# Layout of the per-pixel weights in DRAM: the eight rows of a column side by side, in place of the columns of a row

## The chip, the core and the metric

The kernel runs on one core of one Trainium2 chip. The metric is the device time of one execution, in microseconds (us). It is reported as the median of several runs; beside it stands one execution that was recorded by the hardware profiler, with its own time. A core has a tensor engine (PE, with its weight loads shown as PEld), a vector engine (DVE), a scalar engine (ACT), GpSimd (POOL) and SyncE (SP), which here only issues DMAs. Sixteen DMA engines carry all transfers. Each engine works through its own instructions in order and waits on semaphores.

## What is computed

Two layers on a batch of 32 images, 256 channels, 32x32 pixels, float32. Layer 0 is group norm, a 3x3 convolution with operands rounded to a half-precision format, bias, and a residual sum. Layer 1 is an involution: after a group norm, two 1x1 convolutions make for every pixel a 7x7 kernel for each of 16 groups of 16 channels, and that kernel is applied to the pixel's neighbourhood.

```python
x = x + _L0_conv_ref(_gn(x), weight, bias)            # 3x3, 256 -> 256
xn = _gn(x)
y = relu(batch_norm(einsum('oc,bchw->bohw', w1, xn))) # 256 -> 64
w = einsum('oc,bchw->bohw', w2, y) + b2               # 64 -> 16*49
w = w.reshape(b, 16, 49, H, W)
patches = 7x7 neighbourhoods of xn, (b, 16, 16, 49, H, W)
x = x + einsum('bgkhw,bgckhw->bgchw', w, patches)
```

## The kernel before

The 32 images go through a software pipeline written out by hand. The loop at the end of the function counts steps; an image takes 16 of them (`per = 2 * M`, M = 8), so that at a span of 1342.5 us an image costs about 42 us and a step about 2.6 us. Each stage of an image has a lag in steps (`due(n, lag)`): the front (group norms, convolution, first 1x1 convolution, transposes) runs 56 steps ahead, the per-pixel weights 18 steps ahead, and the sums of the involution at lag 0.

The involution is done on TensorE as products with band matrices. An image is cut into K = 4 bands of TR = 8 rows. A band's matrix needs the 7x7 weights laid out so that partition (r, j) holds, at a place that depends on j, the weights of pixel (row r, column j); the left and the right half of the row (SIDES = 2, JC = 16 columns each) lie behind one another. Getting there takes a trip through DRAM:

1. `weights` (L411) computes the weights of four rows in PSUM; DVE adds the bias and writes them into a ring in SBUF (`evict`, L435): partition = column, the rows as slots of the ring.
2. `scatter` (L476, on SP's queue) writes the ring into the DRAM tensor `wd`, one DMA for each of the 7 column offsets `dj`: 32 columns x 8 rows, pieces of WB = 160 elements (640 B). There are 7 x 4 x 32 = 896 of these DMAs, in two parts of a band (`part` 0: 4 of them, `part` 1: 3, one step later). A piece goes to column p + dj, tap place 6 - dj, so that afterwards the seven pieces of one column and row lie in a run of WPIX = 1128 elements (4512 B).
3. `load_bands` (L497) reads it back: for each j of 0 to 15 one DMA that takes 8 rows x 2 sides, runs of up to 1128 elements, into the 8 partitions `band[j::16]`. j = 0 and 1 go by SP's queue, the other 14 by POOL's. The order in a band is `ORDER`, j = 15 last. A band is loaded 9 steps before its sums; there are three band buffers (NBAND = 3).
4. `sums` (L522) multiplies with the band on PE, `add_windows` (L538) adds to x on DVE, `store` (L543) writes out by SP's queue. `load_x` (L106) fetches images by SP's queue too.

At the beginning three DMAs by SP's queue (L191) put zeros into the parts of `wd` that no scatter writes: the 8 spare elements at the end of every run, and the border columns. Their source is a band buffer that POOL has set to zero.

`wd` before is `[H, S, WPIX]`, with S = 38 columns (32 and a border of 3 on each side): the columns of a row follow one another at 4512 B, and the rows at ROW = S * WPIX elements, 171 KB.

Of the kernel before, what the change touches and what calls it, by code (L numbers as in the profile page):

```python
# [9 lines left out]
F32 = mybir.dt.float32  # L10
# [4 lines left out]
B, C, H, W = 32, 256, 32, 32  # L15
# [5 lines left out]
K1, PAD1 = 7, 3  # L21
# [18 lines left out]
TR = RG * XR  # L40
SIDES = 2
JC = W // SIDES
K = H // TR
# [8 lines left out]
V = 2  # L52
A = G // V
WB = G * WIN
PAD = V * (TR - XR)
WPIX = K1 * WB + PAD
SW = K1 * G
S = H + 2 * PAD1
T = 4
TW = P // T  # L60
PAIR = 3 * GC
PAIRS = G // 2
ROW = S * WPIX
WR = 4
NBAND = 3
BY_SYNC = (0, 1)
# [12 lines left out]
def tile_quant_conv_then_involution(  # L79
# [10 lines left out]
    nc = tc.nc  # L90
# [6 lines left out]
    dram = ctx.enter_context(tc.tile_pool(name="dram", bufs=1, space=bass.MemoryType.DRAM))  # L97
# [44 lines left out]
    bands = [const.tile([P, SIDES, WINC * WB + PAD], F32, name=f"band_{i}") for i in range(NBAND)]  # L142
# [5 lines left out]


    w_sb = const.tile([P, 2, RING, A, WIN, V], F32, name="w_sb")  # L150
    wd = dram.tile([H, S, WPIX], F32, name="wd")
    acc = [ps_acc.tile([P, RG, NT], F32, name=f"acc_{d}") for d in range(SIDES)]

    wq = const.tile([P, CH, K0 * K0, C], F16, name="wq")
# [23 lines left out]
    nc.vector.tensor_sub(bn_shift, bn[:, 1:2], bn_shift)  # L178


    for col, cols, at, n in (
        (0, S, K1 * WB, PAD),
        (PAD1, PAD1, 0, PAD1 * WB),
        (W, PAD1, (K1 - PAD1) * WB, PAD1 * WB),
    ):
        to = bass.AP(
            tensor=wd.tensor,
            offset=wd.offset + col * WPIX + at,
            ap=[[ROW, H], [WPIX, cols], [1, n]],
        )  # L190
        nc.sync.dma_start(to, bands[NBAND - 1][:H, 0, :n].unsqueeze(1).to_broadcast([H, cols, n]))  # L191

    def quantize_weights(kh):

# [270 lines left out]
    def scatter(b, k, part):  # L465

        at = (b * H + k * TR) % RING
        for dj in range(part, K1, 2):
            t, e = divmod(dj, 2)
            to = bass.AP(  # L470
                tensor=wd.tensor,
                offset=wd.offset + k * TR * ROW + dj * WPIX + (K1 - 1 - dj) * WB,
                ap=[[WPIX, TW], [ROW, TR], [1, WB]],
            )
            rows = w_sb[t * TW : (t + 1) * TW, e, at : at + TR]
            nc.sync.dma_start(to, rows.rearrange("p s a r v -> p s (a r v)"))  # L476

    def load_bands(b, k):

        band = bands[(b * K + k) % NBAND]  # L480
        side = WINC * WB + PAD
        for i, j in enumerate(ORDER):
            cut = max(0, PAD1 - j)
            n = (K1 - cut) * WB + PAD
            src = bass.AP(
                tensor=wd.tensor,
                offset=wd.offset + k * TR * ROW + (j + PAD1) * WPIX + cut * WB,
                ap=[[ROW - V, TR], [(W - 1 - 2 * j) * WPIX - cut * WB, SIDES], [1, n]],
            )
            to = band[j::JC]  # L490
            to = bass.AP(
                tensor=to.tensor,
                offset=to.offset + (j + cut) * WB,
                ap=[to.ap[0], [side + (JC - 1 - 2 * j - cut) * WB, SIDES], [1, n]],
            )
            queue = nc.sync if j in BY_SYNC else nc.gpsimd
            queue.dma_start(to, src)  # L497
# [56 lines left out]
    with tc.manual_schedule():  # L554
        fronts = {}
        for n in range(FRONT, B * per + 2):
# [30 lines left out]
            for part in range(2):  # L587
                b, i = due(n, -LEAD + 1 + part)
                if b is not None and i % 2 == 0:
                    for k in range(K):  # L590
                        if i // 2 == min((k + 1) * TR // WR, H // WR - 1):
                            scatter(b, k, part)
# [5 lines left out]
            if b is not None and i % 4 == 0:  # L598
                load_bands(b, i // 4)
# [38 lines left out]
```

## Time and profile before

| | |
|---|---|
| median of 3 runs | 1353.44 us (1347.35 to 1364.31) |
| the profiled execution, its own time | 1344.24 us |
| its span, first to last instruction | 1342.5 us |
| mean granted clock of TensorE | 0.982 |
| PE busy | 1253.6 us (93%) |
| POOL busy | 1014.4 us (76%) |
| DVE busy | 818.8 us (61%) |
| ACT busy | 733.3 us (55%) |
| DMA packets | 360724, 361.85 MB, mean 270 GB/s |

The profiled execution is 0.7% under the median of the runs. "Busy" leaves out the issuing of DMAs on SP; for POOL it includes it (L497 POOL). In a list of waits a line names the engine that waited and its line, then the engine or DMA that ended the wait; the numbers are the microseconds in total, how often, and the longest. In the chain, which is followed back from the last instruction, each piece is what the piece after it had waited for. "SPq" is SP's queue, where each DMA issue has a duration of its own.

### The profile page before, as it was taken

Reading aid. Unit: us, or ns where it says so; the run is one execution under the profiler, and the core shown is the slowest. Engines: PE = TensorE matmul, PEld = TensorE weight load, DVE = VectorE, ACT = ScalarE, POOL = GpSimd, SP = SyncE. Lnnn points to the kernel's source line nnn. Section 1 sums busy time; section 2 is a strip of 40 time slices with the busy share of each in tenths; the row PEclk is TensorE's granted clock in tenths of the full one; section 3 lists DMA queues with packets and bytes.
Section 4 is the critical chain, followed back from the end, with each engine's and each line's share of the span. In section 5 each row is a group of like instructions: output and inputs, shape, how many; then the busy total and the mean of one; then the engine's idle time right before and its main releaser. Section 6 shows DMA issues by size and latency. Waiting matters only on the chain.

```text
span 1342.5 us, 65799 instructions
## 1 busy us (share of the span) xinstructions
PE 1253.6 (93%) x27648; PEld 763.7 (57%) x27648; DVE 818.8 (61%) x2539; ACT 733.3 (55%) x1731; POOL 1014.4 (76%) x1818
## 2 busy tenths in 40 slices
PE   5899999999999999999999999999999999999665
PEld 2356566565555655556655556666555566556454
DVE  3466666565666665656665666766666666666442
ACT  5775656455656556556545655655556564553300
POOL 9067878777787778777778787788777877788785
PEclk9999999999999999999999999999999999999987
DMA  6089999999999999999999999999999999999995
GB/s 228 11 237 295 271 293 293 279 266 281 272 286 282 291 285 270 283 263 280 293 282 283 270 288 282 293 297 296 281 288 275 277 284 290 271 281 266 278 274 166
DMA packets 360724, 361.85 MB, mean 270 GB/s; under 512 B 75056, under 2 KB 304752, under 8 KB 359152
## 3 DMA queue, kind: packets, MB, share of 16 engines
q1 hardware_dynamic: 278512, 229.38, 56.8%
q0 software_dynamic: 81920, 128.28, 33.9%
q8 instruction: 220, 3.60, 1.1%
q14 instruction: 72, 0.59, 0.1%
HBM read 176.60 MB, written 180.76 MB: 266 GB/s over the span
## 4 chain that ended last, share of the span: by engine, by line
PE 60%; DMA 23%; POOL 7%; issue 3%; ACT 3%; DVE 2%; SPq 1%; POOLq 0%; DVEq 0%; ACTq 0%
PE pc L332 25%; PE acc L522 19%; DMA band<-wd 17%; PE pw L411 11%; POOL band L497 7%; DMA wd<-w_sb 6%; PE pt L396 3%; PE py L377 3%; ACT junk L214 1%; SPq L476 1%; DVE w_sb L435 1%; DMA x<-in_x 1%; ACT xn L273 0%; SPq L497 0%; ACT xq L273 0%
## 5 line engine op out<-in xcount | busy, mean ns | idle before, releaser
L497 POOL DMA_DIRECT2D band<-wd x1792 | 980.3, 549 | 315.7 <-DMA band<-wd 182.0
L435 DVE TENSOR_TENSOR w_sb<-pw,late_sb 128x224 f32<-128x224 f32 (+7 forms) x1280 | 330.4, 322 | 419.5 <-PE pw L411 419.2
L332 PE MATMUL pc<-xq,wq 128*128 128x496 f16 (+3 forms) x2304 | 535.2, 379 | 20.3 <-ACT xq L273 18.3
L522 PE MATMUL acc<-band,pixels 64*32 64x190 f32 (+1 forms) x16384 | 426.6, 332 | 51.8 <-DMA band<-wd 42.7
L522 PEld LDWEIGHTS acc<-band,pixels 64*32 64x32 f32 x16384 | 304.7, 107 | 159.7 <-issue 81.1
L332 PEld LDWEIGHTS <-wq 128*128 128x128 f16 x2304 | 206.7, 98 | 316.1 <-issue 102.7
L411 PE MATMUL pw<-late_sb,y 64*32 64x224 f32 (+1 forms) x8192 | 288.9, 333 | 10.8 <-issue 9.4
L538 DVE TENSOR_TENSOR x<-acc,x 128x380 f32<-128x380 f32 (+1 forms) x512 | 262.0, 512 | 32.2 <-PE acc L522 23.2
L411 PEld LDWEIGHTS pw<-late_sb,y 64*32 64x32 f32 x8192 | 186.5, 106 | 38.1 <-issue 21.0
L400 ACT COPY pixels<-pt 128x512 f32<-128x512 f32 x128 | 73.7, 576 | 228.6 <-PE pt L396 228.6
L214 ACT ACTIVATE junk<-x 128x512 f16<-128x512 f32 (+1 forms) x192 | 146.4, 763 | 14.7 <-DVE x L348 12.2
L214 ACT ACTIVATE junk<-x,mean 128x1024 f16<-128x1024 f32 x128 | 147.1, 1149 | 4.3
L245 ACT ACTIVATE s<-back,eps 128x2 f32<-128x2 f32 x64 | 18.9, 296 | 178.6 <-DVE back L230 178.6
L346 DVE TENSOR_SCALAR q<-pc 128x512 f16<-128x512 f32 x128 | 87.2, 681 | 17.6 <-PE pc L332 17.6
L273 ACT ACTIVATE xn<-x,off,rstd 128x512 f32<-128x512 f32 x128 | 96.2, 800 | 0.0
L348 DVE SCALAR_TENSOR_TENSOR x<-q,early_sb,x 128x512 f32<-128x512 f16 x128 | 94.2, 736 | 0.3
L396 PEld LDWEIGHTS pt<-ident,xn 128*128 128x128 f32 x512 | 63.9, 142 | 26.3 <-issue 2.5
L396 PE MATMUL pt<-ident,xn 128*128 128x128 f32 x512 | 78.0, 275 | 0.1
L273 ACT ACTIVATE xq<-x,off,rstd 128x1024 f16<-128x1024 f32 x64 | 75.7, 1227 | 0.0
L235 ACT ACTIVATE mean<-back 128x2 f32<-128x2 f32 x64 | 12.6, 196 | 101.4 <-DVE back L230 101.4
L377 PE MATMUL py<-xn,early_sb 128*64 128x512 f32 x256 | 62.2, 606 | 0.9 <-ACT xn L273 0.9
L224 DVE STREAM_TRANSPOSE across<-sums 128x32 f32<-128x32 f32 x128 | 26.3, 205 | 33.6 <-ACT junk L214 32.4
(40 smaller groups left out, 369.3 us busy)
## 6 DMA issues: line engine op xcount, KB each, us to landing
wd<-w_sb SPq DMA_DIRECT2D x896, 160.0 KB
band<-wd POOLq DMA_DIRECT2D x1664, 70.5 KB, 4.6
x<-in_x SPq DMA_DIRECT2D x64, 512.0 KB
out<-x SPq DMA_DIRECT2D x64, 512.0 KB
band<-wd POOLq DMA_DIRECT2D x128, 60.5 KB, 4.6
band<-wd SPq DMA_DIRECT2D x128, 50.5 KB
band<-wd SPq DMA_DIRECT2D x128, 40.5 KB
band<-in_w SPq DMA_DIRECT2D x2, 1152.0 KB
```

Source lines behind the costliest of these rows:

```text
L214: nc.scalar.activation(junk[:, n0:n1], src[:, h, n0:n1], func, bias=bias, accum_out=self.sums[:, i : i + 1])
L273: nc.scalar.activation(dst, src, AF.Identity, bias=self.off[:, one], scale=self.rstd[:, one])
L332: nc.tensor.matmul(pc.rearrange("p (r c) -> p r c", c=W)[:, r0 - nt * RT : r1 - nt * RT, c0:c1], wq[:, kh, k, mh * P : (mh + 1) * P], xq[: ...
L346: nc.vector.tensor_scalar(q, pc, F16_MAX, -F16_MAX, ALU.min, ALU.max)
L348: nc.vector.scalar_tensor_tensor(xt[:, mh, cols], q, bias_sb[:, mh : mh + 1], xt[:, mh, cols], ALU.add, ALU.add)
L377: nc.tensor.matmul(py[i * CR : (i + 1) * CR], w1_sb[:, kh, :], px[:, :, i], start=kh == 0, stop=kh == CH - 1,)
L396: nc.tensor.transpose(pt[:, i, h * P : (h + 1) * P], xn[:, h, (m + i) * P : (m + i + 1) * P], ident)
L411: nc.tensor.matmul(pws[i][t * TW : (t + 1) * TW, : dj.stop - dj.start, r], y_sb[b % 2][half, (r0 // 2 + r) * W : (r0 // 2 + r + 1) * W], w ...
L435: nc.vector.tensor_tensor(to, of[:, :, d0:d1], bias[:, :, d0:d1], ALU.add)
L497: queue.dma_start(to, src)
L522: nc.tensor.matmul(at[t * TW : (t + 1) * TW, h, :, f - top : l - top], px[p, a, v * GC : v * GC + TW], of[:, :, a, f - top : l - top, v], ...
L538: nc.vector.tensor_tensor(x_at, of, x_at, ALU.add)
```

## The change

`wd` becomes `[K, S, TR, WPIX]`: for each band of 8 rows, the 38 columns follow one another, and within a column the 8 rows lie side by side. Rows of a column are then 4512 B apart (WPIX), columns COL = 8 * 1128 elements = 36,096 B apart, bands BLOCK = 38 * COL apart. A band occupies the same stretch of `wd` as before.

```diff
-ROW = S * WPIX
+COL = TR * WPIX
+BLOCK = S * COL
...
-    wd = dram.tile([H, S, WPIX], F32, name="wd")
+    wd = dram.tile([K, S, TR, WPIX], F32, name="wd")
...
+    zeros = bands[NBAND - 1][:, 0]
     for col, cols, at, n in (
         (0, S, K1 * WB, PAD),
         (PAD1, PAD1, 0, PAD1 * WB),
         (W, PAD1, (K1 - PAD1) * WB, PAD1 * WB),
     ):
         to = bass.AP(
             tensor=wd.tensor,
-            offset=wd.offset + col * WPIX + at,
-            ap=[[ROW, H], [WPIX, cols], [1, n]],
+            offset=wd.offset + col * COL + at,
+            ap=[[BLOCK, K], [WPIX, cols * TR], [1, n]],
         )
-        nc.sync.dma_start(to, bands[NBAND - 1][:H, 0, :n].unsqueeze(1).to_broadcast([H, cols, n]))
+        nc.sync.dma_start(to, zeros[:K, :n].unsqueeze(1).to_broadcast([K, cols * TR, n]))
...
     def scatter(b, k, part):
...
-                offset=wd.offset + k * TR * ROW + dj * WPIX + (K1 - 1 - dj) * WB,
-                ap=[[WPIX, TW], [ROW, TR], [1, WB]],
+                offset=wd.offset + k * BLOCK + dj * COL + (K1 - 1 - dj) * WB,
+                ap=[[COL, TW], [WPIX, TR], [1, WB]],
...
     def load_bands(b, k):
...
-                offset=wd.offset + k * TR * ROW + (j + PAD1) * WPIX + cut * WB,
-                ap=[[ROW - V, TR], [(W - 1 - 2 * j) * WPIX - cut * WB, SIDES], [1, n]],
+                offset=wd.offset + k * BLOCK + (j + PAD1) * COL + cut * WB,
+                ap=[[WPIX - V, TR], [(W - 1 - 2 * j) * COL - cut * WB, SIDES], [1, n]],
```

In the built program the order of the instructions, and the semaphores that each waits for, are the same on all five engines. What differs is the form of some DMAs. The builder joins dimensions that follow one another without a gap: the destination of a scatter, 32 x 8 x 160 before, is 256 x 1 x 160 after (its source stays 32 x 8 x 160); and the load of j = 15, whose two sides were neighbours and made one run of 2256 elements, is 8 x 2 x 1128 after, like the others. The builder also marks each DMA that SP issues as prepared ahead or not. Before, all 896 scatters are marked as prepared; after, none is. The loads of the bands have the mark neither before nor after, and neither has the first of the three fills, whose form is of the same kind as the new scatter's (destination 1216 x 1 x 8, source 32 x 38 x 8). The sources of the fills have 4 partitions in place of 32.

## Prediction

> **What bounds the kernel now.** I read the stretches of the steady part first, to see which resource is full there; then the waits of PE, for what a faster or slower transfer is worth; then SP's issues and waits, because the change alters 896 of SP's instructions; last the chain, to see where they lie on the path.
>
> The steady part, by stretches (length, busy time of PE, PEld, DVE, ACT, POOL, clock, share of the DMA engines, GB/s):
>
> ```profile
> 300.00:600.00 300.00, 288.30 (x6425) 174.74 (x6409) 186.84 (x579) 172.27 (x406) 227.73 (x417) 0.99 0.96 279
> 600.00:900.00 300.00, 294.64 (x6594) 180.19 (x6593) 194.90 (x614) 170.90 (x406) 233.41 (x427) 0.99 0.97 285
> ```
>
> PE is busy 96 to 98% and the DMA engines 96 to 97%: two resources are full together. What makes DMA slower has only 3% to hide in; what makes it faster gains only PE's idle time. Of that, this much ends on a band:
>
> ```profile
> PE acc L522 <- DMA band<-wd: 42.7, 22, 4.6
> ```
>
> So PE waits for a band 22 times in 128 bands, 42.7 us in all: the most that faster transfers of wd can give directly.
>
> What the DMA engines carry, by queue:
>
> ```profile
> q1 hardware_dynamic: 278512, 229.38, 56.8%
> q0 software_dynamic: 81920, 128.28, 33.9%
> ```
>
> Queue 1 (SP) has the scatters. The trace's packet records say more: 229376 packets of 640 B take 32 ns at the median and 35.6 in the mean, 511 us of each engine's 1342; 24576 reads of 4512 B on queue 0 take 174 ns at the median and 239 in the mean.
>
> SP's issues (durations ns min/median/max), lines 191, 476 and 497, and what SP waited for:
>
> ```profile
> L191 SPq DMA_DIRECT2D wd<-band x3: 444/676/3967, 7.7 to 12.5; - x3
> L476 SPq DMA_DIRECT2D wd<-w_sb x896: 302/528/2644, 64.4 to 1310.8; - x180
> L497 SPq DMA_DIRECT2D band<-wd x256: 569/594/1580, 73.7 to 1317.3; - x128
> ...
> SPq L476 <- DVE w_sb L435: 161.4, 68, 48.7
> SPq L106 <- DMA out<-x: 77.1, 27, 4.1
> SPq L476 <- DMA wd<-w_sb: 34.8, 55, 2.2
> ```
>
> By the records the 896 scatter issues sum to 621 us and all of SP's issues to 905 of the span; the rest, some 430 us, SP waits. In only 68 of the 256 parts of bands did SP wait for the eviction (w_sb); in the others the scatter was late already, or came just in time.
>
> The chain, first over the whole span, then one of the places where it runs through the trip to DRAM:
>
> ```profile
> PE 60%; DMA 23%; POOL 7%; issue 3%; ACT 3%; DVE 2%; SPq 1%; POOLq 0%; DVEq 0%; ACTq 0%
> ```
>
> ```profile
> 632.41 1.26 DVE w_sb L435 x4
> 633.67 0.47 DVE x L538
> 634.14 0.04 SPq L476
> 634.18 0.05 issue
> 634.23 0.92 SPq L476
> 635.16 0.05 issue
> 635.21 4.00 DMA wd<-w_sb
> 639.21 0.04 issue
> 639.24 0.55 POOL band L497
> 639.79 4.86 DMA band<-wd
> ```
>
> A loop closes here: weights at 631 us, eviction, scatter, load, and PE takes up the band at 664.5. Two thirds of the chain's time are not in this trip; a third is.
>
> **The change, part by part.**
>
> *Order and waits.* Every instruction keeps its place and its semaphores on all five engines, so no wait is added, none removed, nothing moved past a queue. Cost 0, up or down.
>
> *Scatter issue.* The 896 scatters lose the builder's mark "prepared ahead". In this trace the unmarked DMAs on SP are the loads of L497, never under 569 ns, and the first fill, 676 ns (the first of L191: the three take 5.17 us from 7.73, the last two 4.46 from 8.45). That fill is the nearest row: same pair of forms, a one-level destination from a two-level source. The marked scatter takes 302 alone and under 442 in a quarter of the cases (records); its median 528 already contains waiting for a full queue. So the price is 676 - 442 = 234 ns each; ends 148 (against the median) and 374 (against the minimum). A gain is excluded: no unmarked issue is under 569. Over 896 that is 210 us of SP's time (133 to 335), which SP's 430 us of waits hold. If they didn't, see the second rival. What shows is what lies on the chain: over the whole span it holds some 25 scatter issues of 0.29 us or more, 16.1 us together. At 0.234 each: +5.9 us (ends 3.7 and 9.4). Where an issue took over 0.68 already (8 of the 25), the queue was full and the new price hides in it; raising only the shorter ones to 0.676 gives +3.8. I take **+5 us**.
>
> *Scatter transfer.* Same 256 pieces of 640 B. The 256 places of one scatter are at one even pitch of 4512 B now; before they were 8 stretches, 171 KB apart, of 32 such places. The nearest row for writes at that even pitch is the first fill: 1216 packets of 32 B at 4512 B, 9 ns each, no more than a 4-byte packet (9 ns). So 0. Ends: the mean falls to the median, (35.6 - 32) x 229376 / 16 = 51 us less work per DMA engine; or rises as much, 51 us more. I take 0 because the median is all payload and a fixed part (20 B per ns, 26 in the 4512-B reads), with nothing left that an address could shorten.
>
> *Band reads.* The same runs of up to 4512 B; the eight rows now come from 36 KB in one piece. What could fall is the mean over the median: 65 ns x 24576 / 16 = 100 us per engine. But the reads of x, whose rows are neighbours in DRAM already, show the same excess: 4096 B, median 159, mean 207 ns (30% against 37%). So the excess comes from sharing the engines, not from the rows' distance: 0, ends -100 and, by symmetry, +100 us of engine work.
>
> *j = 15.* 1024 reads of 9024 B (mean 459 ns) become 2048 of 4512 (2 x 239): 19 x 1024 / 16 = 1.2 us of engine work; POOL's issue stays at 0.55 us. 0.
>
> *Fills.* The packet records have 16 landings for each of the three fills; with 4 source partitions I price them on 4 engines: 1216 x 9 ns / 4 = 2.7 us in place of 0.7, and 96 packets of 1920 B (mean 112 ns) / 4 = 2.7 in place of 0.7, twice: 6 us later. They are issued by 12.9 us and the first scatter at 64.4, so 51 us of convolution cover it; the loads of x behind them are for images 2 and 3. Cost 0; without cover +6.
> The Trainium skill, page "DMA: Bandwidth & Descriptors", section "Why a DMA increments its semaphore by 16 and not by 1", says that a DMA runs on the largest number of engines, at most 16, that divides the slowest dimension of both sides. By it the scatters stay on 16 engines (32 and 256) and the fills fall to 4, which speaks against this change only at the start; the sum by it is the same, and no run here shows it yet.
>
> **Sum.** Profiled execution 1344.2 + 5 = 1349.2. It lies 0.7% under the median of the runs shown, so for a median: 1353.4 + 5 = **1358 us**.
>
> **The rivals.**
>
> 1. *Nothing shows*: SP's queue is so often held by full DMA rings (issues up to 2644 ns) that the longer issue disappears. Against it: 59% of the scatter issues are under 600 ns. Time 1353.
>
> 2. *SP sets the pace (slower).* The place is part 1 of a band: three scatters behind the eviction, each +0.234 us, 0.70 us per band, 128 bands: 90 us if every band were bound. The trip's share of the chain (DMA, POOL, SP and the eviction, about 34%) makes it +30: **1384**. For it: 188 of 256 parts found SP late or just in time, and SP's load goes from 905 to 1115 us of 1342. Against it: PE waits for only 22 bands. It decides once SP's 430 us of waits are used up: 430 / 896 = 0.48 us more per scatter, an issue of some 0.9 us.
>
> 3. *DRAM likes the new neighbours (faster).* Half the excess of the reads goes, 50 us per engine, DMA falls from 97 to some 93%, and half to all of PE's 42.7 us vanish: 1311 to 1332. Against it: the reads of x above.
>
> 4. *DRAM dislikes the new pitch (slower).* Writes go to 40 ns in the mean: 4.4 x 229376 / 16 = 63 us per engine, of which 3% of the steady 1140 us, 35 us, find room: 1381 to 1416. Against it: the fill's 9 ns.
>
> **How the numbers follow.** Forecast 0.50 (1358; its own range 1347 to 1372), rival 1 0.18, rival 2 0.17, rival 3 0.08, rival 4 0.07. The range leaves out rival 3 but for its top (0.07), rival 4 (0.07) and the upper part of rival 2 (0.06): 1333 to 1390. About 2% is what a measurement of this kernel can tell from no change: 1326 and 1381. Faster by more: 0.06, most of rival 3. Slower by more: 0.12 of rival 2, 0.06 of rival 4, 0.01 of the forecast: 0.19. Within: 0.75.
>
> **What would show it.** Right: L476's minimum and median on SP near 600 to 700 ns; the steady DMA share and packet count (about 1000 more) as before; PE's wait for bands near 43 us, SP's wait for w_sb down by some 100 us or more. Wrong: a DMA share or GB/s that moves by over 2 points (rivals 3, 4, or other engine counts); PE's wait for bands over 70 us with SP hardly waiting (rival 2); an issue near 1 us, or scatters landing later than the 4.00 us shown.

## The result, and the profile after

| | before | after |
|---|---|---|
| median of 20 runs | 1354.33 us (1344.98 to 1364.31) | 1360.70 us (1351.09 to 1371.53) |
| ratio | | 1.0046, interval 1.0024 to 1.0068 |
| profiled execution, its own time | 1344.24 us | 1351.09 us |
| its span | 1342.5 us | 1349.3 us |

The kernel is a half per cent slower, clear of the measurement's noise and far inside 2%. In a second set of runs, together with the first experiments and all on one chip, the same pair gave 1.0089 (1.0059 to 1.0119). So the size of the loss is known only to lie between a quarter of a per cent and one and a quarter; its sign is not in doubt. The prediction was 1358 us.

The scatters after, by the view of line 478 (which was 476; durations in ns, min/median/max), and what SP then waited for:

```profile
L478 SPq DMA_DIRECT2D wd<-w_sb x896: 549/634/2631, 67.2 to 1317.4; - x180
...
SPq L478 <- DVE w_sb L437: 98.1, 75, 35.6
SPq L107 <- DMA out<-x: 73.7, 27, 4.4
...
SPq L478 <- DMA wd<-w_sb: 14.0, 30, 2.5
```

The least issue went from 302 to 549 ns and the median from 528 to 634. SP's wait for the evictions shrank from 161.4 to 98.1 us. SP waited for them about as often as before (75 times in place of 68), but for less time; in the stretch from 120 to 1260 us, without the start, it was 96.3 us before and 50.3 after. By the trace's records the 896 issues sum to 720 us in place of 621, and all of SP's issues to 1019 in place of 908.

The full resources, in the same stretches as before, show no more work and a little less pace:

```profile
300.00:600.00 300.00, 287.42 (x6434) 176.56 (x6418) 187.13 (x579) 172.62 (x407) 229.97 (x421) 0.99 0.95 278
600.00:900.00 300.00, 291.36 (x6493) 176.54 (x6485) 191.16 (x602) 169.34 (x401) 230.72 (x424) 0.99 0.96 280
```

The DMA share is a point lower, 0.95 and 0.96 for 0.96 and 0.97. Longer transfers at the same pace would have raised it. POOL's waits show where the delay is passed on; in the stretch from 120 to 1260 us, first before, then after:

```profile
POOL band L497 <- DMA band<-wd: 171.2, 219, 2.9
...
POOL band L497 <- DMA wd<-w_sb: 22.5, 24, 3.1
```

```profile
POOL band L499 <- DMA band<-wd: 155.3, 184, 4.6
POOL band L499 <- DMA wd<-w_sb: 50.1, 39, 5.0
```

The wait for a scatter to land more than doubled. Part of it only replaces another wait (for earlier loads, 171.2 before, 155.3 now). PE's wait for bands hardly moved over the whole span of this execution (42.7 before), and the chain still goes through PE for most of its length (63%):

```profile
PE acc L524 <- DMA band<-wd: 44.6, 20, 5.6
```

2.8 of the 6.8 us between the two spans arise before the first sums (87.68 us before, 90.46 after) and have another origin, which comes at the end.

### The profile page after: what moved, and what is told of

It reads as the page before. It is cut to its first block, busy times and chain, and to the rows that moved or that the text cites. A ratio compares the mean times of both kernels' runs of the same rounds, so it can differ in the third digit from the quotient of the medians.

```text
span 1349.3 us, 65799 instructions
## 1 busy us (share of the span) xinstructions
PE 1248.7 (93%) x27648; PEld 762.6 (57%) x27648; DVE 826.2 (61%) x2539; ACT 734.1 (54%) x1731; POOL 1011.3 (75%) x1818
## 4 chain that ended last, share of the span: by engine, by line
PE 63%; DMA 20%; POOL 4%; DVE 4%; issue 3%; ACT 3%; SPq 2%; POOLq 0%; DVEq 0%; ACTq 0%
PE pc L334 25%; PE acc L524 21%; DMA band<-wd 12%; PE pw L413 12%; DMA wd<-w_sb 7%; POOL band L499 4%; PE pt L398 3%; PE py L379 3%; DVE w_sb L437 2%; SPq L478 1%; ACT junk L216 1%; DVE x L540 1%; DVE wq L197 1%; DMA band<-in_w 1%; ACT xn L275 0%
## 5 line engine op out<-in xcount | busy, mean ns | idle before, releaser
L524 PE MATMUL acc<-band,pixels 64*32 64x190 f32 (+1 forms) x16384 | 426.0, 331 | 60.2 <-DMA band<-wd 44.6
L413 PE MATMUL pw<-late_sb,y 64*32 64x224 f32 (+1 forms) x8192 | 282.6, 332 | 7.8 <-issue 6.2
## 6 DMA issues: line engine op xcount, KB each, us to landing
band<-wd SPq DMA_DIRECT2D x128, 40.5 KB
```

Of the source, the lines that this page charges most:

```text
L413: nc.tensor.matmul(pws[i][t * TW : (t + 1) * TW, : dj.stop - dj.start, r], y_sb[b % 2][half, (r0 // 2 + r) * W : (r0 // 2 + r + 1) * W], w ...
L524: nc.tensor.matmul(at[t * TW : (t + 1) * TW, h, :, f - top : l - top], px[p, a, v * GC : v * GC + TW], of[:, :, a, f - top : l - top, v], ...
```

## The experiments

Theory 1: the scatters lost the mark "prepared ahead", their issue on SP takes longer, the scatters land later, and through POOL's queue the bands come later. Theory 2: the order of the addresses in DRAM makes reads or writes dearer. Theory 3: the fills, or what else differs at the start. All ratios are against the kernel before, run on the same chip. The first four runs share the chip of the second set above; the halves and the move of a load to POOL share another chip, and the last four runs another again.

**The mark alone.** The layout, the fills and the forms of before:

```diff
+            nc.dge_precook = False
             nc.sync.dma_start(to, rows.rearrange("p s a r v -> p s (a r v)"))
+            nc.dge_precook = True
```

> The kernel before, with its old layout, old fills and old forms, where the 896 scatters alone lose the mark 'prepared ahead'. Theory 1 (the longer issue on SP, on the way from the weights to the band, is the whole cost): ratio to before as for the change, 1.0046, with the scatter issue's median near 634 ns and SP's wait for the evictions down from 161 us towards 100. Theory 2 (the order of addresses in DRAM costs time): 1.000. Theory 3 (the fills, or what else differs at the start, cost the time): 1.000.

Measured: 1.0048 (1.0015 to 1.008), 1359.75 us. The view of the line:

```profile
L477 SPq DMA_DIRECT2D wd<-w_sb x896: 556/636/2374, 63.5 to 1321.0; - x180
...
SPq L477 <- DVE w_sb L435: 97.8, 57, 47.5
```

The issue (median 636) and the wait for the evictions (97.8 us) are those of the changed kernel, without any address moved, and the interval excludes that the mark costs nothing. Whether it is the whole loss depends on what it is set against: it equals the 1.0046 of the first set of runs, but on the chip of this run the changed kernel lost more (1.0089, below), 12.1 us at the medians against 7.7 here.

**The layout alone.** A ninth, unused row behind each column keeps the builder from joining the dimensions:

```diff
-COL = TR * WPIX
+TRS = TR + 1
+COL = TRS * WPIX
...
-    wd = dram.tile([K, S, TR, WPIX], F32, name="wd")
+    wd = dram.tile([K, S, TRS, WPIX], F32, name="wd")
```

(The fills clear the spare rows too.)

> The kernel after with a ninth, unused row behind the eight of each column, so that the columns are 40.6 KB apart and the builder can't join the dimensions: the rows of a column still lie side by side, the scatters have the old form and the mark again, the fills stay on few engines. Theory 1: ratio to before 1.000, scatter issue's median back near 528 ns. Theory 2: 1.0046 with the issue back near 528. Theory 3: 1.002 to 1.0046.

Measured: 1.0014 (0.9982 to 1.0046), 1355.38 us; issue median 525 ns, minimum 302. No loss that can be told from zero, though this run alone does not exclude a loss of up to 0.46% from the layout, or from the new fills and the split load of j = 15, which this kernel has too. The packets speak against a loss by the layout: pieces of 640 B took 35.8 ns in the mean here and 35.2 in the changed kernel (35.6 before), reads of 4512 B 237 and 240 ns (239 before).

**The fills alone undone.** The changed kernel with zeros from 32 and 24 partitions:

```diff
-        nc.sync.dma_start(to, zeros[:K, :n].unsqueeze(1).to_broadcast([K, cols * TR, n]))
+    nc.sync.dma_start(
+        to.rearrange("(p c) n -> p c n", c=S), zeros[: K * TR, :PAD].unsqueeze(1).to_broadcast([K * TR, S, PAD])
+    )
...
+        nc.sync.dma_start(to, zeros[: PAD1 * TR, :n].unsqueeze(1).to_broadcast([PAD1 * TR, K, n]))
```

> The kernel after, whose three fills take their zeros from 32, 24 and 24 partitions in place of 4. Theory 1 and theory 2: ratio to before 1.0046. Theory 3: 1.000 to 1.002, with the first sums back at 87.7 us from the start in place of 90.5, and the quantizing of the weights on DVE back at 1.8 us in place of 4.3 and 6.2.

**The changed kernel again**, on the same chip:

> The kernel after once more, for a second profile of it on the same chip as the others. If the slow start (quantizing on DVE 4.3 and 6.2 us, first sums at 90.5 us) belongs to the change, it is there again; if it is chance, it comes and goes, in kernels with and without the new fills. Ratio to before 1.0046 by every theory.

Measured: 1.0059 (1.0026 to 1.0093) without the new fills, 1.0089 (1.0059 to 1.0119) with them. The intervals overlap; a third of a per cent from the fills can be neither shown nor excluded. The loss remains without the new fills, and with the first sums back at 87.7 us, so theory 3 is not the main cause. In the repeat the quantizing took 1.7 us twice and the first sums came at 87.39 us: the slow start was not there, though the fills were.

These four profiles and the first two can be set side by side. The waits in the stretch from 120 to 1260 us, in microseconds:

| kernel | scatters | SP for the evictions | POOL for a scatter to land | PE for a band or a scatter |
|---|---|---|---|---|
| before | marked | 96.3 | 22.5 | 17.5 |
| spare row | marked | 93.6 | 19.9 | 13.4 |
| mark alone removed | unmarked | 34.0 | 43.4 | 23.4 |
| after | unmarked | 50.3 | 50.1 | 21.4 |
| after, again | unmarked | 40.5 | 51.2 | 27.5 |
| after, fills undone | unmarked | 40.4 | 58.7 | 31.9 |

Each step of theory 1 follows the mark, in the old layout and in the new one: SP waits less for its input, POOL waits longer for the scatters, PE waits longer for the bands. So the mark is shown to be a cause, and the way that the delay takes is seen. That it is the only cause is not shown: on this chip the change lost 0.6 to 1.2%, the mark alone 0.15 to 0.8%, and everything but the mark (the spare row) between a gain of 0.2% and a loss of 0.5%.

**A larger dose of issue.** Each scatter as two DMAs of 16 columns, in both layouts:

```diff
+            for c in range(0, TW, TW // 2):
...
-                ap=[[WPIX, TW], [ROW, TR], [1, WB]],
+                    ap=[[WPIX, TW // 2], [ROW, TR], [1, WB]],
...
-            rows = w_sb[t * TW : (t + 1) * TW, e, at : at + TR]
+                rows = w_sb[t * TW + c : t * TW + c + TW // 2, e, at : at + TR]
```

> The kernel before with each scatter as two DMAs of 16 columns, still marked as prepared: 1792 issues. If a marked issue costs 0.3 to 0.44 us alone, a pair costs about what a median scatter of before takes with its waiting for a full queue, 0.6 to 0.9 us. Theory 1: ratio to before 1.005 to 1.02. A theory in which the issue on SP doesn't matter: 1.000. It is the control for the next run.

> The kernel after with each scatter as two DMAs of 16 columns, not marked: at 549 ns at least, a pair is over 1.1 us, past the 0.9 us at which the prediction let SP's waits run out. Theory 1 with that bound: SP has next to nothing left to wait for, PE's wait for bands goes over 100 us, ratio to before 1.04 to 1.10, and far above the run with marked halves. If the issue is hidden by full DMA queues, as the prediction's first rival has it: within 0.01 of the marked halves.

Measured: 1.2018 (1.1966 to 1.2069) with marked halves, 1.3371 (1.3308 to 1.3434) with unmarked ones. Both expectations of theory 1 were far too low in size. The two views, marked halves first:

```profile
L477 SPq DMA_DIRECT2D wd<-w_sb x1792: 302/442/2603, 63.6 to 1603.9; - x200
```

```profile
L479 SPq DMA_DIRECT2D wd<-w_sb x1792: 549/599/2346, 67.1 to 1791.3; - x200
```

SP's issues sum to 1231 and 1467 us, of spans of 1627 and 1817. Between the two kernels that is 236 us more issue for 183 us more time, 0.78 us for each, although SP still waited for a fifth of the span or more. PE then waits for scatters and loads alike; in the kernel with marked halves:

```profile
PE acc L523 <- DMA band<-wd: 130.9, 45, 8.3
PE acc L523 <- DMA wd<-w_sb: 121.9, 30, 7.7
```

The halves also changed the transfers (640-B packets 41.7 and 46.4 ns in the mean), but the DMA share fell from 0.96 to 0.86 and 0.81 (120 to 1260 us), so the DMA engines were not the full resource. TensorE's mean granted clock was lower too, 0.923 and 0.878 in place of 0.982. What twice the number of DMAs costs apart from their issue was not separated.

**SP relieved of one load.** `BY_SYNC = (1,)`: the load of j = 0 goes to POOL.

> The kernel before with the load of j = 0 on POOL's queue in place of SP's: SP loses 128 issues, 90 us in all, nearly what the change added to it; POOL gains 128 x 0.55 = 70 us and goes from 76% to 81%. Theory 1: if SP's load costs time in the kernel before already, 0.995 to 1.000, unless POOL's longer queue takes it back (1.000 to 1.01). Where SP's load plays no part: 1.00 to 1.01.

> The kernel after with the load of j = 0 on POOL's queue: takes off SP what the change put on it. Theory 1: the ratio to before comes back from 1.005 to 1.009 towards 1.000, by more than the same move does to the kernel before. If SP's load as such plays no part and only the delay of the single scatter does: as the kernel after, 1.005 to 1.009, or more through POOL.

Measured: 1.0487 (1.0443 to 1.0531) for the old layout, 1.0341 (1.0299 to 1.0382) for the new one. Relieving SP cost 68 us in the first: POOL got 128 more issues of 0.55 us, 70 us, and about as much is added to the time. That is far outside what was expected. It reads as if POOL's queue were a bound of its own, though POOL is "busy" 76% only; no run shows that by itself. That the changed kernel lost less, 1.5 points less, was not expected either.

**SP given one load more.** `BY_SYNC = (0, 1, 2)`:

> The kernel before with a third load (j = 2) moved from POOL's queue to SP's: SP gains 128 issues of 0.6 to 0.9 us, 77 to 115 us, as much as the change added to it; POOL loses 72 us. Theory 1 alone (SP's issue time costs, POOL's doesn't): 1.005. If, as moving a load to POOL showed (68 us more for 70 us of issue), POOL's queue costs one for one too: 0.95 to 1.00, better than both kernels.

> The kernel after with the same third load on SP's queue. SP then issues about 1120 us of the span and waits little. Theory 1, with SP's waits running out: worse than the run before it by clearly more than the change's 0.5 to 0.9%, by 2 to 5%. If SP's issue were hidden behind POOL or the DMA engines: the difference stays at 0.5 to 0.9% or less.

Measured: 1.0106 (1.0066 to 1.0145) and 1.0418 (1.0366 to 1.047). SP's issues: 1004 and 1090 us. The first is no better than either kernel, and both of its expectations missed. In it POOL's wait for scatters to land, from 120 to 1260 us, is 120.0 us in place of 22.5: what POOL gains in issue it seems to lose in waiting for SP. The second shows what the change costs where SP has less room: 3.1 points (theory 1 had 2 to 5) in place of 0.5 to 0.9, for 86 us more issue. SP's own waits in it, from 120 to 1260 us:

```profile
SPq L107 <- DMA out<-x: 54.6, 27, 3.4
SPq L478 <- DVE w_sb L437: 23.5, 43, 1.3
```

**Why the change cost less where POOL had the load of j = 0.** Layout or issue:

> The spare-row kernel (new neighbourhood in DRAM, old marked issue) with the load of j = 0 on POOL. It is to tell why, with that load on POOL, the kernel after was faster than the kernel before (1.034 against 1.049). Theory A (the new layout itself, or the form of the load of j = 15, helps where POOL's loads set the pace): 1.034. Theory B (the longer issue of the scatters helps there, by spacing them): 1.049.

> The kernel before with the scatters unmarked and the load of j = 0 on POOL: old layout, longer issue. Theory A (the layout helps): 1.049 or a little more. Theory B (the longer issue helps by spacing the scatters): 1.034.

Measured: 1.0519 (1.0474 to 1.0563) with the new layout and the short issue, 1.0398 (1.0359 to 1.0436) with the old layout and the long issue. So here too the issue decides and the layout doesn't, as theory B had it. A longer issue on SP makes this variant about 1% faster (1.0398 against 1.0519 on the same chip, and against 1.0487 for the old layout with the short issue on another). How it helps was not shown: the spacing of the scatters is only a name for it.

## Why the prediction was right

*Order and waits.* Cost 0, as said: 65799 instructions in both profiles.

*Scatter issue.* The mechanism is shown: the mark alone gives 1.0048. The single terms were off and made up for one another. The price of 234 ns was too high for most issues. The shortest grew by 247 ns (302 to 549), but the first quartile by 159 (442 to 601), the median by 106 and the mean by 110 (693 to 803). The fill's 676 ns was a poor stand-in: an unmarked scatter took 601 at the first quartile. Issues that were long already hardly grew (one in ten took over 1241 ns before, over 1313 after), as the prediction said of those on the chain. Over all of SP the growth is 111 us, not 210.

The part that reached the time, +5 us, was read from the chain of one execution, and chains differ much. Of scatter issues of 0.29 us or more, the chain holds 25 before and 8 in the spare-row kernel, whose issues are as short; at 0.234 us each that would have been +1.9 in place of +5.9. The runs gave 6.4 us in the first set and 12 in the second. That +5 hit the first so closely is in good part luck; 2.8 us of the profile's own 6.8 were the slow start, which no step foresaw. Two sums were slightly off and do not change the forecast: by the records the 25 issues sum to 15.2 us, not 16.1, and SP's issues to 908, not 905.

*Scatter transfer.* 0, as said: 35.6 ns before, 35.2 after.

*Band reads and j = 15.* 0, as said: 4512-B reads 239 ns before, 240 after, though eight rows now come from one piece of 36 KB. Packets rose by 2012, not about 1000, because a 4-byte packet came with each of the 1024 new ones.

*Fills.* The 4-byte packets of SP's queue fell by 36, 3 x (16 - 4), and in the run with 24 source partitions for the two border fills by 8, 2 x (16 - 12). So the fills run on 4 engines, as the Trainium skill ("DMA: Bandwidth & Descriptors", "Why a DMA increments its semaphore by 16 and not by 1") has it: each engine that such a DMA uses reports its own end. The size was wrong: a packet of 1920 B took 285 ns in place of 112, and the two border fills ran some 15 us, not 5.4. The loads of x behind them were held up, on SP too (before, the three fills took 5.17 us of SP and the four loads 2.75):

```profile
7.74 9.55 SPq L193 DMA_DIRECT2D wd<-band  x3
17.33 14.20 SPq L107 DMA_DIRECT2D x<-in_x  x4
```

All that ended by 38 us, and the first scatter in the repeat came at 64.1 us: the cover held.

*Rival 1* (nothing shows) fails by the interval of 1.0048. *Rival 2* (SP sets the pace) has the right place but a wrong bound: it let all of SP's 430 us of waits be room. With one load more on SP the changed kernel issues only 182 us more than the kernel before, SP still waits 307 us, and the kernel is already 4.2% slower. A likely reading is that mainly the wait for the evictions is room: from 120 to 1260 us it was 96 us before and 23.5 there, while the 77 us for a store to land before x is loaded gave up only 22. No run separates the two. *Rivals 3 and 4* fail by the packet times and by the spare row, as far as its interval reaches.

*The signs.* PE's wait for bands (44.6 us), the DMA share and the median issue (634 ns) came as the prediction said. The shortest issue (549 ns) lies under its 600 to 700, and SP's wait for the evictions fell by 63 us, not by 100 or more.

## What to carry to other kernels

A DMA has two costs, the transfer and the issue, and a change of layout can leave the first as it is and raise the second. Look at the form that the builder makes of both sides of a DMA: dimensions that lie without a gap in memory are joined, here on one side only; the DMA lost its mark with it, and its issue took 247 ns more at the least and 110 ns more in the mean. Not all the time in which a queue waits is room: ask first how long it waits for the input of the very work that is to be late (here some 100 us of 430), though that alone did not give the size of the loss. Moving work off a queue (here to POOL, 70 us of issue for 68 us of time) can cost more than it relieves. And a share read from the chain of one execution is a weak base for a small effect: waits that move together in several profiles show it better.

## What was not expected of the hardware

*Two courses of the start.* DVE's quantizing of the convolution's weights (two operations of 128 x 2304) took 1.8 us each in the profile before, and in the profile after:

```profile
8.66 4.35 DVE L197 TENSOR_SCALAR wq<-band 128x2304 f16<-128x2304 f32 x1 [1.03 <-DMA band<-in_w]
...
14.03 6.22 DVE L197 TENSOR_SCALAR wq<-band 128x2304 f16<-128x2304 f32 x1
```

The second lies beside a memset of POOL, in the same profile:

```profile
13.06 5.98 POOL L198 MEMSET band<- 128x7056 f32 x1 [1.27 <-DVE wq L197]
```

In the fast course POOL's memsets are stretched instead (two of the six small ones took 1.94 us in place of 0.73). In all 14 profiles each of DVE's two operations ends 1.21 to 1.23 us after the last memset that ended before it: in the slow course after all six small ones or the large one, in the fast course between two small ones, of which the later is then stretched by 1.2 us. It looks as if the two engines took turns, one waiting until the other is through; no run tests that. Which of the two gets its way differs between profiles: the slow course stands in 4 of the 7 profiles whose fills read 4 partitions, and in none of the other 7. Whether the fills favour it is open; it moved the first sums by about 3 us.

*Few source partitions.* The border fills' packets of 1920 B took 112 ns in the mean when 32 partitions were read by 16 engines, and 285 ns when 4 partitions were read by 4.

*POOL's loads.* With 128 more issues of 0.55 us on POOL's queue the kernel was 68 us slower, though the busy share shows a quarter of POOL's time idle.
